# Groups of 6, 7, 6 and 6 destination blocks in an attention layer, and a rearranged passage into it

## The chip, the cores and the metric

The kernel runs on one core of one Trainium2 chip. The metric is the device time of one execution in microseconds. The median of three runs of the kernel before is 1526.83 us (1523.18 to 1527.76).

## What is computed

A graph network with four layers on 3125 nodes of 128 features and 103,125 edges, sorted by destination; behind each layer the input is added back and a layer norm follows. The change is at the passage from layer 0 to layer 1:

```python
# layer 0: a weighted sum over edges
xw = x @ weight
out = relu(segment_sum(edge_val[:, None] * xw[src], dst, N) + b)
x = layernorm(x + out)

# layer 1: attention, 4 heads of 32 features
h = (x @ W).reshape(n, HEADS, C)
a_s = einsum('nhc,hc->nh', h, att_src)
a_d = einsum('nhc,hc->nh', h, att_dst)
e = leaky_relu(a_s[src] + a_d[dst], 0.2)
p = exp(e - segment_max(e, dst)[dst])
alpha = p / (segment_sum(p, dst)[dst] + 1e-16)
out = segment_sum(h[src] * alpha[:, :, None], dst)
out = out.reshape(n, 128) + gat_bias + x @ skip_W + skip_b
x = layernorm(x + layernorm(out) * ln_g + ln_b)
```

Layer 2 is attention without edge features, layer 3 two mean aggregations with dense products.

## The kernel before

The nodes are cut into 25 blocks of 128 (`NB`). A first stage turns the edges into two dense matrices in DRAM, source block by destination block: `wd`, the sums of edge weights in float32, and `f_ctd`, the number of edges in bfloat16. All four layers then run as dense products over these matrices on TensorE.

**The sums of layer 0.** `add0` (L803) takes one source block `i`: it loads the weights of that block for a range of destination blocks into a tile `cw` (up to ten blocks, 640 KB) and adds `cw^T @ xw[i]` onto one accumulator per destination block; four blocks share a PSUM bank. A float32 product counts as two matmuls in the profile. PSUM has eight banks: five (`acc0` to `acc4`) hold the first twenty destination blocks (`Z0`), which are summed while the matrices are still being made; at the end of the stage the loop L931 adds those source blocks that are still missing. Only then are the banks of the stage free, and the last five destination blocks are summed in `left0` and `left1` by the loop at L1192, over all 25 source blocks, from tiles of a pool of its own (`f_tp1`, eight tiles of 320 KB), which lies in SBUF where pools of the first stage lay. `end0` (L818) applies bias, relu and the layer norm to a bank.

**What is hung into that loop.** `marks` lists steps by source block. `scores1(g)` (L1111) turns four blocks of x, multiplies them with the attention vectors into bank `tr_sa` and a second bank, and sends the second result to DRAM (`add_`). `top` copies the scores to SBUF (`heads`, L1127) and finds their maximum; `spread` and `factors` (L1136) make the exponentials of the nodes (`fa`, `fb`, `own1`) from it. `values(b)` (L1156) makes the features of two source blocks: a product, two scalings on DVE (L1165), and a split into three bfloat16 parts (`split3`, L553 to L561: three casts on ACT, two subtractions on DVE), then negations on DVE (L1175). Four calls of `values` stand in the loop, at source blocks 13, 16, 19 and 22; the remaining nine stand in the first pass of layer 1.

**Layer 1.** `IG` (L503) cuts the destination blocks into groups of 4, 7, 7 and 7. For each group and each pair of heads one pass runs over the 25 source blocks. For a source block, `masks` (L1234) makes one 0/1 mask for each head over the group's columns: for one of five a single DVE operation (L1250), for the others a Relu on ACT (L1256) and a minimum on DVE (L1257). `products` (L1261) then issues three matmuls for each destination block, one with the counts (L1267) and two with the masks (L1272). A destination block has a PSUM bank of its own, 402 floats. At the end of a pass `sums` (L1285) reduces each bank on DVE (`nz`, L1291), so the next pass's products into a bank wait for that. `quotients`, `finish1` (two layer norms, gain, bias, and the products that layer 2 needs) and `skips` are put a number of steps later with `later`, one step being one source block; they run beside the masks and products of later passes. For the first group, the banks of layer 0 are used: two of its sums and two of left; for later groups seven banks and one spare.

**The order.** A scheduler arranges the instructions of each engine around the program's order; each engine and each queue runs in its order. SP issues all loads and stores of this stretch from one queue, so a load that waits for a tile holds those behind it.

Of the kernel before, what the change touches and what calls it, by code (L numbers as in the profile page):

```python
# [7 lines left out]
F32 = mybir.dt.float32  # L8
# [7 lines left out]
P = 128  # L16
N = 3125
NB = 25
# [476 lines left out]
NBT = NW // BW  # L495
LW = 4
NL = (NBT - 1) * BW + LW
Z0 = 20
V1 = 100
GA = 80.0  # L500
UP = 2.0**60
GM = 40.0
IG = [(0, 4), (4, 7), (11, 7), (18, 7)]  # L503
QG = [(0, 13), (13, 12)]
LN = N - (NB - 1) * P
GT = [(0, 4), (4, 4), (8, 4), (12, 4), (16, 4), (20, 2), (22, 2), (24, 1)]
# [4 lines left out]
def fast_path(  # L511
# [287 lines left out]
    def bias0(acc, n):  # L799
        for j in range(n):  # L800
            nc.tensor.matmul(acc[:, j, :], ones, l0_br, start=(j == 0), stop=False, skip_group_check=True)

    def add0(pool, i, accs, blocks):  # L803

        b0, n = blocks
        for h in range(0, n, 10):
            m = min(10, n - h)
            cw = pool.tile([P, min(10, n), P], F32, name="cw")[:, 0:m]
            nc.sync.dma_start(
                cw.rearrange("p c d -> p (c d)"), wd[i * P : (i + 1) * P, (b0 + h) * P : (b0 + h + m) * P]  # L810
            )
            for j in range(h, h + m):
                nc.tensor.matmul(  # L813
                    accs[j // 4][:, j % 4, :], cw[:, j - h, :], xw[:, i, :], start=False,
                    stop=(i == NB - 1 and (j % 4 == 3 or j == n - 1)), skip_group_check=True,
                )
# [61 lines left out]
    for b in range(NBT):  # L878
# [49 lines left out]
        while acc0 and (done + 1) * P <= (b - 1) * BW * WN:  # L928
            add0(zp, done, acc0, (0, Z0))
            done += 1  # L930
    for i in range(done, NB):  # L931
        add0(zp, i, acc0, (0, Z0))
    front.close()
    r = xw

# [20 lines left out]
    def later(k, f):  # L956
        due.append((now[0] + k, f))
# [123 lines left out]
    with ExitStack() as st:  # L1081
# [16 lines left out]

        fp = st.enter_context(tc.tile_pool(name="f_fp1", bufs=2))
        tail = ExitStack()  # L1100
        tp = tail.enter_context(tc.tile_pool(name="f_tp1", bufs=8))
        zpp = zero.enter_context(tc.tile_pool(name="f_zpp", bufs=1, space=PSUM))
        left = GB[Z0 // 4 :]
        acc1 = [zpp.tile([P, 4, P], F32, name=f"left{k}") for k in range(len(left))]
        t8 = zpp.tile([P, 512], F32, name="tr_sa")
        for a, (b0, n) in zip(acc1, left):
            bias0(a, n)
        for g in range(Z0 // 4):
            end0(acc0[g], *GB[g])

        def scores1(g):  # L1111

            b0, n = GB[g]
            tag = f"acc{min(g, 2)}"
            turned(zps, xT, b0, n, tag)
            for k in range(n):
                b = b0 + k
                nc.tensor.matmul(
                    t8[:, b * 2 * H : (b + 1) * 2 * H], xT[:, b * P : (b + 1) * P], watt, start=True, stop=True
                )  # L1120
# [6 lines left out]
        def heads(b0, n):  # L1127

            b = slice(b0, b0 + n)
            nc.vector.tensor_copy(  # L1130
                sa[:, b, :], t8[:, b0 * 2 * H : (b0 + n) * 2 * H].rearrange("p (b h) -> p b h", h=2 * H)
            )
            nc.vector.tensor_scalar(nas[:, b], sa[:, b, 0:H], -1.0, None, OP.mult)
            nc.gpsimd.tensor_scalar(bas[:, b], sa[:, b, 0:H], UP, None, OP.mult)

# [41 lines left out]
                )  # L1177

        spare.append(lambda: zps.tile([P, 512], F32, name="few", tag="acc1"))
        marks = {3: lambda: scores1(0), 4: lambda: (scores1(1), scores1(2)), 5: lambda: scores1(3), 6: lambda: scores1(4)}  # L1180
        keep = {}

        def top():
            heads(0, Z0)
            ex = fp.tile([P, H], F32, name="ex", bufs=1)
            nc.vector.tensor_reduce(ex, sa[:, 0:Z0, 0:H].rearrange("p b h -> p h b"), AX.X, OP.max)
            keep["d"] = highest(fp, ex, H)

        marks[7] = top
        marks[9] = lambda: (spread(keep["d"], H, km), factors(0, Z0))  # L1190
        ready = 0
        for i in range(NB):  # L1192
            add0(tp, i, acc1, (Z0, NB - Z0))
            if i in marks:
                marks[i]()
            if i >= 13 and i % 3 == 1:
                values(ready)
                ready += 2
        tail.close()
# [85 lines left out]
        def sums(acc, g, hp):  # L1285
# [469 lines left out]
```

## Time and profile before

| | |
|---|---|
| median of three runs | 1526.83 us |
| the profiled execution | 1523.26 us |
| its span, first to last instruction | 1521.5 us |
| TensorE busy | 1387.3 us, 91% |
| DVE busy | 975.9 us, 64% |
| ACT busy | 903.8 us, 59% |
| last product of the edge matrices (L901) | starts at 468.1 us |
| last product of the first twenty sums | ends at 498.2 us |
| maximum of the scores known (`km`) | 528.45 us |
| last product of left | starts at 544.1 us |
| first product of layer 1 | 546.6 us |
| reductions `nz` of the eight passes begin | 597.4, 627.3, 685.5, 732.1, 793.6, 841.9, 903.3, 955.1 us |
| first products of scores in layer 2 (L1408) | 962.0 us |

PE is TensorE's matmul side, PEld its weight loads, DVE, ACT and POOL the other engines, SPq the queue that issues DMAs. In a row of a stretch the columns are the stretch, its length, and for each engine its busy time with the number of instructions; then the granted TensorE clock as a share of full speed, the share of time that the 16 DMA engines were busy, and the rate. In a row of the timeline the start, the duration, engine, line and operation, output<-inputs and the count are given; brackets hold the idle time before it and what ended it. In a row of a group, busy time and the mean of one follow the first bar, and idle time before it with its causes follows the second.

### The profile page before, as it was taken

To read this page: it belongs to the slowest core of one execution; us is meant where nothing else is said; L and a number is where in the kernel's file an instruction comes from. 1 tells how busy PE (TensorE), PEld (TensorE's weight loads), DVE (VectorE), ACT (ScalarE), POOL (GpSimd) and SP (SyncE) were. 2 spreads that over 40 slices of the span, in tenths; PEclk is the share of its full clock that TensorE was granted. 3 is DMA by queue.
4 is the path that set the end of the run, shared out by engine and by line. 5 is a ranking of instruction groups with operands and counts; after the bars stand their busy time and mean duration, and the time that the engine had idled before them with its cause. 6 is when DMAs were issued, how large, how long until landed. Compare 5 with 4: busy or idle time off the path is not lost. (4 is left out here: it accounts for less than half of the span.)

```text
span 1521.5 us, 35026 instructions
## 1 busy us (share of the span) xinstructions
PE 1387.3 (91%) x14762; PEld 1214.9 (80%) x14775; DVE 975.9 (64%) x1595; ACT 903.8 (59%) x1845; POOL 129.3 (8%) x164
## 2 busy tenths in 40 slices
PE   2898999999997987899989989899999999999994
PEld 2898999899897776889979979677777774458994
DVE  5989999989990389869978878544464351012006
ACT  2878887878882479878778677454465331023003
POOL 2000000000000023113212311300000000000000
PEclk9999999999999999999999999999999999999997
DMA  6478787877888633444434433332222216513651
GB/s 172 125 194 217 211 225 189 241 200 208 230 229 253 201 101 98 143 122 123 133 117 120 130 92 104 123 111 68 68 61 78 80 62 251 200 36 133 199 191 46
DMA packets 209702, 223.92 MB, mean 147 GB/s; under 512 B 72956, under 2 KB 183339, under 8 KB 209277
## 3 DMA queue, kind: packets, MB, share of 16 engines
q1 hardware_dynamic: 208748, 218.51, 49.5%
q8 instruction: 117, 1.92, 0.5%
q0 software_dynamic: 400, 1.97, 0.4%
q10 hardware_dynamic: 385, 1.11, 0.3%
q14 instruction: 52, 0.43, 0.1%
HBM read 157.19 MB, written 64.36 MB: 146 GB/s over the span
## 5 line engine op out<-in xcount | busy, mean ns | idle before, releaser
L1272 PE MATMUL acc<-vp,cm 128*128 128x198 bf16 x2500 | 343.2, 252 | 7.3 <-DVE cm L1257 4.6
L1256 ACT ACTIVATE fm<-adr,bas 128x896 bf16<-128x896 f32 (+1 forms) x320 | 286.0, 952 | 66.6 <-DVE cm L1257 61.9
L1267 PE MATMUL acc<-vp,ct 128*128 128x204 bf16 x1250 | 314.1, 255 | 8.3 <-DVE vp L1175 4.5
L1272 PEld LDWEIGHTS <-cm 128*128 128x128 bf16 x2500 | 235.1, 98 | 25.2 <-DVE cm L1257 8.6
L901 PE MATMUL wp<-wod,ohc 128*128 128x128 bf16 x3768 | 242.1, 220 | 10.0 <-ACT cs L906 5.5
L901 PEld LDWEIGHTS <-ohc 128*128 128x128 bf16 x3768 | 222.0, 98 | 11.9 <-issue 11.6
L862 DVE TENSOR_TENSOR wod<-ohd,w 128x4096 bf16<-128x4096 bf16 (+2 forms) x122 | 221.3, 1867 | 0.6 <-PE wp L901 0.6
L1257 DVE TENSOR_TENSOR cm<-fm,ct 128x896 bf16<-128x896 bf16 (+1 forms) x320 | 196.7, 644 | 36.1 <-PE acc L1272 13.8
L868 ACT ACTIVATE wod<-ohd,wu 128x128 bf16<-128x128 bf16 x628 | 194.5, 399 | 0.0
L1412 DVE TENSOR_TENSOR e<-e,ct 128x416 f32<-128x416 f32 (+1 forms) x175 | 108.2, 625 | 106.8 <-ACT e L1411 99.3
L1411 ACT ACTIVATE e<-s,f_nm 128x416 f32<-128x416 f32 (+1 forms) x175 | 109.5, 632 | 98.4 <-PE s L1408 91.3
L1416 PEld LDWEIGHTS acc<-self__8021,e 128*128 128x128 f32 x1250 | 148.5, 193 | 20.5 <-issue 18.5
L1416 PE MATMUL acc<-self__8021,e 128*128 128x129 f32 x1250 | 149.0, 276 | 0.5 <-DVE e L1412 0.5
L1408 PE MATMUL s<-yT,f_xT 128*128 128x416 f32 (+1 forms) x350 | 142.6, 542 | 4.6 <-ACT rt L1388 4.0
L813 PE MATMUL acc<-f_xw,cw 128*128 128x128 f32 x1000 | 119.4, 279 | 8.0 <-DMA cw<-wd 8.0
L1267 PEld LDWEIGHTS <-ct 128*128 128x128 bf16 x1250 | 122.2, 98 | 2.4 <-issue 1.5
L813 PEld LDWEIGHTS acc<-f_xw,cw 128*128 128x128 f32 x1000 | 115.4, 194 | 8.8 <-DMA cw<-wd 8.8
L912 ACT COPY ws<-wp 128x512 f32<-128x512 f32 x157 | 91.5, 583 | 48.7 <-PE wp L901 43.2
L893 PE MATMUL cp<-ohc,ohd 128*128 128x125 bf16 x1256 | 96.7, 219 | 23.9 <-ACT ws L912 14.7
L851 DVE TENSOR_TENSOR ohd<-kd,ramp 128x4096 bf16<-128x4096 bf16 (+1 forms) x41 | 90.0, 2196 | 28.2 <-PE cp L893 27.9
L1408 PEld LDWEIGHTS s<-yT,f_xT 128*128 128x128 f32 x350 | 62.3, 191 | 55.4 <-issue 39.4
L1591 PEld LDWEIGHTS <-ct 128*128 128x128 bf16 x1875 | 104.9, 98 | 0.0
(301 smaller groups left out, 1483.8 us busy)
## 6 DMA issues: line engine op xcount, KB each, us to landing
ct<-f_ctd SPq DMA_DIRECT2D x48, 800.0 KB
wd<-ws SPq DMA_DIRECT2D x39, 896.0 KB
ct<-f_ctd SPq DMA_DIRECT2D x150, 224.0 KB
cw<-wd SPq DMA_DIRECT2D x50, 640.0 KB
f_ctd<-cs SPq DMA_DIRECT2D x20, 1000.0 KB
ct<-f_ctd SPq DMA_DIRECT2D x25, 416.0 KB
ct<-f_ctd SPq DMA_DIRECT2D x25, 365.2 KB
cw<-wd SPq DMA_DIRECT2D x25, 320.0 KB
```

What stands on the lines that cost most here:

```text
L813: nc.tensor.matmul(accs[j // 4][:, j % 4, :], cw[:, j - h, :], xw[:, i, :], start=False, stop=(i == NB - 1 and (j % 4 == 3 or j == n - 1)) ...
L862: nc.vector.tensor_tensor(packed(f, ww), packed(ohd, ww), twos(w2[s])[:, ww], OP.mult)
L868: nc.scalar.activation(wod[2][:, BW + w, :], ohd[:, BW + w, :], AF.Copy, scale=w3[:, 1, at : at + 1])
L901: made = nc.tensor.matmul(wp[:, j, :], ohc[:, w, :], wod[s][:, w, :], start=(j == 0 and q == 0 and s == 0), stop=(j == 3 and q == 1 and s ...
L1256: nc.scalar.activation(f[:, : n * P], at, AF.Relu, bias=bas[:, c, h : h + 1], scale=UP)
L1257: nc.vector.tensor_tensor(m[:, : n * P], f[:, : n * P], ct[:, : n * P], OP.min)
L1267: nc.tensor.matmul(out_(F1, PW), ct[:, k * P : (k + 1) * P], vp[:, c, hp : hp + 2, :, 2 * F1 : V1], start=(c == 0), stop=False, skip_group ...
L1272: nc.tensor.matmul(out_(0, 2 * F1)[:, j], ms[j][:, k * P : (k + 1) * P], vp[:, c, hp + j, :, 0 : 2 * F1], start=False, stop=(c == NB - 1 a ...
L1408: nc.tensor.matmul(s[:, :m], xT[:, c * P : (c + 1) * P], yT[:, i0 * P + a : i0 * P + a + m], start=True, stop=True)
L1411: nc.scalar.activation(e[:, a : a + m], s[:, :m], AF.Exp, bias=nm[:, q : q + 1], scale=scale)
L1412: nc.vector.tensor_tensor(e[:, a : a + m], e[:, a : a + m], ct[:, a : a + m], OP.mult)
L1416: nc.tensor.matmul(acc[k // 3][:, (k % 3) * (P + 1) : (k % 3 + 1) * (P + 1)], es[q, c][:, k * P : (k + 1) * P], vo[:, c, 0 : P + 1], start ...
```

## The change

- The groups are 6, 7, 6 and 6. The first group takes six banks: `acc3`, `acc4`, `acc2`, `tr_sa` and the two of left.
- `add0` gets the width of a tile as a parameter. The missing source blocks of the first twenty sums (23 and 24, since the loop of the stage reaches 22) are added after the stage's pools are closed, from tiles of five blocks of `f_tp1`. That pool is placed on the other side of SBUF.
- Ahead of these two source blocks the first five source blocks of left are added (`ZA`), and the loop over left begins at the sixth.
- The marks move up by five source blocks, so that they have the same distance from the loop's new begin. `values` runs at every source block from 16 on: nine calls instead of four.
- The scores of the last five blocks go to the bank `acc0` instead of `tr_sa`, and `heads` for them runs within `scores1`.
- The quotients of the first group come seven steps after the pass instead of four.

```diff
+ZA = 5
-IG = [(0, 4), (4, 7), (11, 7), (18, 7)]
+IG = [(0, 6), (6, 7), (13, 6), (19, 6)]
...
-    def add0(pool, i, accs, blocks):
+    def add0(pool, i, accs, blocks, w=10):
...
-        for h in range(0, n, 10):
-            m = min(10, n - h)
-            cw = pool.tile([P, min(10, n), P], F32, name="cw")[:, 0:m]
+        for h in range(0, n, w):
+            m = min(w, n - h)
+            cw = pool.tile([P, w, P], F32, name="cw")[:, 0:m]
...
-    for i in range(done, NB):
-        add0(zp, i, acc0, (0, Z0))
     front.close()
...
-        tp = tail.enter_context(tc.tile_pool(name="f_tp1", bufs=8))
+        tp = tail.enter_context(tc.tile_pool(name="f_tp1", bufs=8, side="right"))
...
         for a, (b0, n) in zip(acc1, left):
             bias0(a, n)
+
+        for i in range(done, NB - 2):
+            add0(tp, i, acc0, (0, Z0), 5)
+        for i in range(ZA):
+            add0(tp, i, acc1, (Z0, NB - Z0), 5)
+        for i in range(max(done, NB - 2), NB):
+            add0(tp, i, acc0, (0, Z0), 5)
...
-            tag = f"acc{min(g, 2)}"
+            tag = f"acc{min(g, 2) if b0 < Z0 else 1}"
             turned(zps, xT, b0, n, tag)
+            t, a = (t8, b0) if b0 < Z0 else (zps.tile([P, 512], F32, name="tr_s", tag="acc0"), 0)
...
+            if b0 >= Z0:
+                heads(t, b0, n)
...
-        marks = {3: lambda: scores1(0), 4: lambda: (scores1(1), scores1(2)), 5: lambda: scores1(3), 6: lambda: scores1(4)}
+        marks = {8: lambda: scores1(0), 9: lambda: (scores1(1), scores1(2)), 10: lambda: scores1(3), 11: lambda: scores1(4)}
...
-        marks[7] = top
-        marks[9] = lambda: (spread(keep["d"], H, km), factors(0, Z0))
+        marks[12] = top
+        marks[14] = lambda: (spread(keep["d"], H, km), factors(0, Z0))
...
-        for i in range(NB):
-            add0(tp, i, acc1, (Z0, NB - Z0))
+        for i in range(ZA, NB):
+            add0(tp, i, acc1, (Z0, NB - Z0), 5)
             if i in marks:
                 marks[i]()
-            if i >= 13 and i % 3 == 1:
+            if i >= 16:
                 values(ready)
                 ready += 2
...
-        later(7, lambda: (heads(Z0, NB - Z0), factors(Z0, NB - Z0)))
+        later(7, lambda: factors(Z0, NB - Z0))
...
-            later(1 if last else 4, quotients)
+            later(1 if last else 4 if g else 7, quotients)
...
-                    acc = [zps.tile([P, 512], F32, name="acc1", tag=f"acc{3 + k}") for k in range(2)]
-                    acc += [zpp.tile([P, 512], F32, name="acc1", tag=f"left{k}") for k in range(2)]
+                    acc = [zps.tile([P, 512], F32, name="acc1", tag=f"acc{k}") for k in (3, 4, 2)]
+                    acc += [zpp.tile([P, 512], F32, name="acc1", tag=k) for k in ("tr_sa", "left0", "left1")]
```

More of the change, by code (lines that the diff above doesn't have):

```diff
@@ L1113, in scores1 @@
             b0, n = GB[g]
-            tag = f"acc{min(g, 2)}"
+            tag = f"acc{min(g, 2) if b0 < Z0 else 1}"
             turned(zps, xT, b0, n, tag)
+            t, a = (t8, b0) if b0 < Z0 else (zps.tile([P, 512], F32, name="tr_s", tag="acc0"), 0)
             for k in range(n):
-                b = b0 + k
                 nc.tensor.matmul(
-                    t8[:, b * 2 * H : (b + 1) * 2 * H], xT[:, b * P : (b + 1) * P], watt, start=True, stop=True
-                )
+                    t[:, (a + k) * 2 * H : (a + k + 1) * 2 * H], xT[:, (b0 + k) * P : (b0 + k + 1) * P], watt,
+                    start=True, stop=True,
+                )
+            if b0 >= Z0:
+                heads(t, b0, n)
             t = zps.tile([P, 512], F32, name="tr_ad", tag=tag)
@@ L1125, in scores1, with heads @@
             nc.sync.dma_start(add_[:, b0 * P : (b0 + n) * P], ad[:, : n * P])
-        def heads(b0, n):
+        def heads(t, b0, n):
             b = slice(b0, b0 + n)
-            nc.vector.tensor_copy(
-                sa[:, b, :], t8[:, b0 * 2 * H : (b0 + n) * 2 * H].rearrange("p (b h) -> p b h", h=2 * H)
-            )
+            nc.vector.tensor_copy(sa[:, b, :], t[:, 0 : n * 2 * H].rearrange("p (b h) -> p b h", h=2 * H))
             nc.vector.tensor_scalar(nas[:, b], sa[:, b, 0:H], -1.0, None, OP.mult)
@@ L1179, in fast_path @@
         spare.append(lambda: zps.tile([P, 512], F32, name="few", tag="acc1"))
-        marks = {3: lambda: scores1(0), 4: lambda: (scores1(1), scores1(2)), 5: lambda: scores1(3), 6: lambda: scores1(4)}
+        marks = {8: lambda: scores1(0), 9: lambda: (scores1(1), scores1(2)), 10: lambda: scores1(3), 11: lambda: scores1(4)}
         keep = {}
         def top():
-            heads(0, Z0)
+            heads(t8, 0, Z0)
             ex = fp.tile([P, H], F32, name="ex", bufs=1)
```

## The prediction

> **What bounds the kernel now.** I read the page's busy shares first, then busy time by stretch, with the stretches cut at the places where the change acts, then the timeline of TensorE in the passage, then the mask operations by shape. All times are of the profiled execution.
>
> ```profile
> span 1521.5 us, 35026 instructions
> PE 1387.3 (91%) x14762; PEld 1214.9 (80%) x14775; DVE 975.9 (64%) x1595; ACT 903.8 (59%) x1845; POOL 129.3 (8%) x164
> ```
>
> TensorE is busy 91% of the span, so a gain must come out of the other 9%, about 134 us, or out of work that disappears. No matmul disappears here. So I ask where TensorE waits.
>
> ```profile
> core 0: us, PE busy (x) PEld busy (x) DVE busy (x) ACT busy (x) POOL busy (x), PEclk, DMA share, GB/s
> 468.40:498.20 29.80, 21.68 (x171) 20.91 (x170) 3.67 (x22) 2.24 (x4) 1.45 (x2) 0.94 0.81 253
> 498.20:528.50 30.30, 29.07 (x199) 22.89 (x200) 9.67 (x51) 13.60 (x33) 0.43 (x1) 0.94 0.70 223
> 528.50:546.60 18.10, 16.76 (x150) 16.59 (x150) 12.49 (x33) 9.14 (x18) 4.74 (x17) 1.00 0.54 159
> 546.60:597.40 50.80, 40.19 (x351) 33.53 (x352) 47.57 (x140) 48.19 (x89) 13.48 (x25) 0.93 0.29 86
> 597.40:627.30 29.90, 28.03 (x308) 26.82 (x307) 27.34 (x68) 27.11 (x42) 5.38 (x7) 1.00 0.46 134
> 627.30:685.50 58.20, 50.88 (x530) 48.74 (x529) 42.99 (x93) 47.00 (x65) 10.54 (x11) 0.97 0.43 128
> 685.50:732.10 46.60, 45.83 (x523) 45.59 (x521) 41.51 (x61) 37.39 (x40) 11.90 (x7) 1.00 0.47 136
> 732.10:793.60 61.50, 53.75 (x556) 50.88 (x554) 49.87 (x108) 47.18 (x68) 15.23 (x10) 0.97 0.39 117
> 793.60:841.90 48.30, 47.61 (x535) 46.93 (x533) 43.22 (x65) 38.06 (x47) 11.33 (x8) 1.00 0.45 130
> 841.90:903.30 61.40, 53.41 (x551) 50.46 (x549) 49.39 (x109) 47.46 (x70) 15.22 (x10) 0.97 0.36 102
> 903.30:955.10 51.80, 48.15 (x537) 47.12 (x535) 41.74 (x65) 31.94 (x41) 10.96 (x8) 1.00 0.34 96
> ```
>
> The rows from 546.6 on are the eight passes of layer 1 (two head pairs for each of four groups), cut where the reductions nz of a pass begin. The first pass (four blocks) has 300 products and takes 50.8 us; DVE and ACT are both busy for some 48 us of it, so these two bound it, with the features (`values`) on top of the masks. The pass 685.5 to 732.1 is bound by TensorE: 525 products in 46.6 us, 0.088 us each, 6.6 us for a block. Passes in which the group before is being finished (58.2, 61.5, 61.4) take 12 to 15 us over that rate.
>
> ```profile
> 471.68 4.73 PE L813 MATMUL acc<-f_xw,cw 128*128 128x128 f32 x40 [1.17 <-DMA cw<-wd]
> 479.00 4.73 PE L813 MATMUL acc<-f_xw,cw 128*128 128x128 f32 x40 [2.59 <-DMA cw<-wd]
> 487.36 10.83 PE L813 MATMUL acc<-f_xw,cw 128*128 128x128 f32 x80 [3.62 <-DMA cw<-wd]
> ...
> 503.53 6.61 PE L813 MATMUL left<-f_xw,cw 128*128 128x128 f32 x50
> ```
>
> The last four source blocks of the first twenty sums wait 7.4 us for their counts; then TensorE mostly idles between 498.2 and 503.5, since SP issued the first load for the five left blocks only at 498.21, when the last reader of the older buffers was through. A full-speed round of left is 10 matmuls of 0.113 us.
>
> ```profile
> L1257 DVE TENSOR_TENSOR cm<-fm,ct 128x896 bf16<-128x896 bf16 x240 | 164.2, 714 | 32.8 <-PE acc L1272 11.8 <-ACT fm L1256 9.5 <-issue 4.5
> L1250 DVE SCALAR_TENSOR_TENSOR cm<-adr,nas,ct 128x896 bf16<-128x896 f32 x60 | 74.9, 1248 | 6.4 <-PE acc L1272 6.3
> L1257 DVE TENSOR_TENSOR cm<-fm,ct 128x512 bf16<-128x512 bf16 x80 | 32.6, 435 | 3.2 <-PE acc L1272 2.0 <-ACT fm L1256 1.1
> L1250 DVE SCALAR_TENSOR_TENSOR cm<-adr,nas,ct 128x512 bf16<-128x512 f32 x20 | 15.7, 786 | 0.7 <-PE acc L1272 0.5 <-DMA ct<-f_ctd 0.2
> L1256 ACT ACTIVATE fm<-adr,bas 128x896 bf16<-128x896 f32 x240 | 233.6, 1032 | 64.1 <-DVE cm L1257 59.5 <-DVE mv L994 3.3 <-DVE ms L1004 0.9
> L1256 ACT ACTIVATE fm<-adr,bas 128x512 bf16<-128x512 f32 x80 | 52.4, 711 | 2.5 <-DVE cm L1257 2.4
> ```
>
> These masks overlap when they stand back to back; from start to start the timeline gives 0.33 and 0.54 us (L1257 at 512 and 896 columns), 0.66 and 1.07 (L1250), 0.61 and 0.93 (L1256). At 768 columns I interpolate 0.47, 0.93 and 0.83.
>
> **What the Trainium skill says.** "TensorE: Matmul & The Clock Gate" (Part 1) says that an idle window of about 3.4 us halves the clock, and that about 3.4 us of work restores it. The trace agrees: the granted clock falls to 0.94 and 0.93 in the stretches with waits and is 1.00 in the pass without. "PSUM — Partial Sum Buffer" (The four PSUM rules) says that a matmul's output stays within one bank; a block here takes 402 floats, so six blocks need six banks, and two of these come late: tr_sa and the second left. "DMA: Bandwidth & Descriptors" (Queues, rings and completion order) says each DMA engine consumes descriptors in ring order; the trace agrees as far as 470 to 490 shows 343 and 302 GB/s at a share of 1.03, so loads put ahead push others back. "ScalarE: Activation LUTs" (What ACT_TABLE_LOAD costs) prices an ACTIVATE with a pointer operand at 280 ns + 0.833 ns per column, less 93 ns back to back, 827 ns at 768 columns, an estimate that fits my 0.83.
>
> **The change part by part.**
>
> *Five rounds of left moved ahead of blocks 23 and 24.* Their loads are 5 x 320 KB = 1.6 MB, 4.8 us at 343 GB/s, in a stretch where DMA is full; they can't fill the waits for free. Block 23's first 640 KB let TensorE start at 487.4; a tile of half the size does so at about 486.5. Then 50 matmuls (5.7 us) and 80 (9.1 us), with the DMA now ahead: the first twenty sums end at about 501.3 instead of 498.2, with five rounds done. Loads go on meanwhile, since the pool now lies on the other side and has eight tiles for both uses; the idle behind 498.2 goes. SP issues eight loads for blocks 23 and 24 instead of four: 4 x 0.43 us of issue, hidden behind 1.1 us of TensorE for each tile (1.7 us if not).
>
> *Scores and maximum.* From the order of the built instructions, 70 matmuls of left stand between that end and km, where 62 stood, and two of values have moved up. 140 x 0.113 (two passes each) = 15.8, five scores of 2.6 (transposes 0.5, two kinds of products 1.06 and 1.02) = 13, values 0.5: 29.3. km stands at about 531 instead of 528.45, with six rounds of left still to do instead of twelve or thirteen. The DMAs of add_ stand in SP's queue behind loads that wait for tiles, and ACT's next copy of ad waits for them; each has 2 to 3 us of TensorE work to hide in, and costs up to 2 if that is short. The counts of the first masks no longer wait for the last tiles of left (1.35 us at 546.6 before); DVE is later than that now, so nothing comes of it. The last two scores copy their heads themselves: one copy and one negation more on DVE, 0.4 us, in the sum below, and one small operation on POOL, which is idle.
>
> *Nine pairs of features before the first mask instead of four.* One pair costs DVE 2.4 us net (two v 0.33, two subtractions 0.68 and 0.64, two negations 0.22) and ACT 1.7. The built order puts all nine, and nearly all of the norm of the left banks, ahead of the first mask on DVE. Start 2.4, nine pairs 21.6, norm and first mask about 4: first masked products at 531 + 28 = 559 instead of 549.4. TensorE has 30 matmuls of left (6.8) and 18 of values (4.5) for these 28 us and idles some 17.
>
> *First pass with six blocks.* TensorE: 450 x 0.088 = 39.5, features of the last seven blocks 1.8, second scores 3.0: 44.3, plus 1.7 for a half clock of 3.4 us behind the idle time. DVE: 42 x 0.47 + 10 x 0.93 = 29.0, four pairs 9.6, the rest (factors, copies, norm) 3.8: 42.4. So TensorE and DVE are almost level, and ACT is not far off; I add 1.5 for their waits on each other (0 to 6 possible). End: 559 + 47.5 = 606.5 instead of 597.4, **9.1 us later**.
>
> *The other seven passes.* They hold 44 block passes instead of 46: 2 x 6.6 = 13.2 us less. Finishing costs, over the TensorE rate, 12.2 us for four blocks and 15.4 for seven, so 1.1 a block on a fixed 7.8: groups of 6, 7, 6 give 14.4 + 15.5 + 14.4 less 0.5 for fewer skips = 43.8 against 43.1. The finish of the first group starts three steps later (quotients after 7, not 4) and spills into its next pass; the three spills I price at 1.7 more. Sum **-10.8** (-13 to -6).
>
> *The end.* Six banks to reduce instead of seven before layer 2 (one nz, 0.57) and one block less to finish beside it (0.6): **-1.2**.
>
> Sum: 9.1 - 10.8 - 1.2 = -2.9. The profiled execution took 1523.26 us (span 1521.5), which would become 1520.4; it lies 3.6 under the median of the runs, 1526.83, from which I get 1524.
>
> **The rivals.** (a) *The new order hides more than I say*: features and masks mesh without waits, the clock does not fall, the passes finish at the old extra cost. First products at 557, pass of 44.5, end 601.5 (+4); rest -13; end -1.2: -10, 1517. For it: DVE had only 3 us of idle in the pass 546.6 to 597.4. Against: three engines over 90%. (b) *Slower: the features become a chain.* ACT has to do five masks (0.83 each) among the last features, and a pair's three casts and two subtractions alternate between ACT and DVE; if a pair takes 3.3 us instead of 2.4, nine take 8.1 longer, TensorE idles 25 us and nothing later gives it back: -2.9 + 8.1 = +5.2, 1532. It decides from a pair of 2.4 + 2.9/9 = 2.7 us on. For it: single-file, the chain v to negation is about 5 us (530.85 to 535.7 in the trace). Against: the built order interleaves two pairs. (c) *It does not fill the waits at all*, because DMA is full: then the sums end 3 us later still, 1527, no change.
>
> **How the numbers follow.** My forecast 0.45, (a) 0.28, (b) 0.17, (c) 0.10. A measurement of this kernel tells apart about 0.3%, 4.6 us. Faster by more: most of (a), and the better third of my own case, 0.27 + 0.15 = 0.42. Slower by more: most of (b), little of the others, 0.17. Between: 0.41. Range: the low end takes in (a) and its spread, the high end (b): 1515 to 1533.
>
> **What would show it.** Right: no wait for cw over 3 us behind the first left load; km near 531; a hole of about 17 us in TensorE before products at 559; nz of the first pass at 606; the other passes at about 44, 60, 48, 55, 42, 54 and 44 us. Wrong: nz before 602 (then masks and features mesh better) or after 611 (the features are a chain), or finishing passes that cost more than 16 us over the rate.

## The result, and the profile after

The kernel after takes 1527.74 us in the median of 12 runs (1525.62 to 1530.84); the kernel before, in 12 runs between them, 1525.43 us (1522.25 to 1528.16). The ratio is 1.0019, 95% interval 1.0011 to 1.0028: slower by 2.9 us, a small but resolved loss. The profiled execution of after took 1530.31 us, that of before 1523.26. This pair is 7.0 us apart, more than the medians, because the one lies 2.6 above its median and the other 2.2 below. So places are read from the profiles, and sizes of a few microseconds from the ratios. The edge matrices are done at another time in each profile (their last product starts at 468.2 us in before and 469.0 in after); where that matters I count from there.

First the busy shares of after, then busy time by stretch, cut at the same events as for before: last product of the edge matrices, first product of left, end of the first twenty sums, `km`, first masked product, and then the beginning of each pass's reductions.

```profile
span 1528.5 us, 35039 instructions
PE 1386.7 (91%) x14762; PEld 1217.6 (80%) x14775; DVE 984.3 (64%) x1597; ACT 905.7 (59%) x1845; POOL 129.0 (8%) x165
```

```profile
469.20:492.30 23.10, 12.51 (x92) 11.95 (x91) 0.09 (x2) 1.87 (x2) 1.45 (x2) 0.88 0.93 279
492.30:509.30 17.00, 17.00 (x132) 17.00 (x133) 3.48 (x19) 0.33 (x2) 0.00 (x0) 0.86 0.91 302
509.30:538.00 28.70, 28.59 (x218) 23.90 (x218) 9.73 (x51) 13.47 (x33) 0.43 (x1) 1.00 0.60 190
538.00:566.20 28.20, 13.33 (x99) 11.69 (x98) 27.59 (x73) 22.35 (x38) 12.01 (x30) 0.74 0.17 57
566.20:614.50 48.30, 46.54 (x473) 44.03 (x474) 42.80 (x100) 45.47 (x69) 5.64 (x13) 0.94 0.41 115
614.50:657.20 42.70, 40.66 (x450) 39.52 (x448) 38.41 (x73) 35.20 (x42) 8.14 (x7) 1.00 0.43 124
657.20:717.60 60.40, 52.83 (x546) 49.58 (x544) 48.08 (x101) 47.36 (x65) 14.64 (x10) 0.97 0.42 121
717.60:768.20 50.60, 48.16 (x534) 47.12 (x533) 43.34 (x65) 38.13 (x48) 10.35 (x8) 1.00 0.43 120
```

TensorE's busy time in the span is the same as before to 0.6 us (1386.7 and 1387.3). The whole difference is waiting. In the first row TensorE idles 10.6 of 23.1 us; in the fourth it idles 14.9 of 28.2 us while DVE is busy all but 0.6 us. The remaining four passes take 57.1, 45.2, 53.8 and 40.9 us.

| us, profiled executions | before | predicted | after |
|---|---|---|---|
| first product of left | 503.5 | 486.5 | 492.3 |
| end of the first twenty sums | 498.2 | 501.3 | 509.3 |
| `km` | 528.45 | 531 | 538.0 |
| first masked product | 549.4 | 559 | 566.2 |
| first `nz` of the first pass | 597.4 | 606.5 | 614.5 |
| the other seven passes together | 357.7 | 346.9 | 350.6 |
| from the last pass's `nz` to the end of the span | 566.4 | 565.2 | 563.4 |

The difference of 7.0 is 17.1 us up to the first `nz`, less 7.1 in the seven passes, less 3.0 behind. The prediction lost its 8 us ahead of the end of the first twenty sums (0.8 of them because the matrices were done later in this execution); from there to the first `nz` it has 105.2 us, and 105.2 were measured. Here is TensorE's timeline of that place (start, duration, operation, count, and in brackets the idle time ahead of it):

```profile
472.52 4.73 PE L814 MATMUL acc<-f_xw,cw 128*128 128x128 f32 x40 [1.20 <-DMA cw<-wd]
479.85 6.36 PE L814 MATMUL acc<-f_xw,cw 128*128 128x128 f32 x40 [2.60 <-DMA cw<-wd]
492.28 8.06 PE L814 MATMUL left<-f_xw,cw 128*128 128x128 f32 x50 [6.08 <-issue]
500.17 9.10 PE L814 MATMUL acc<-f_xw,cw 128*128 128x128 f32 x80
```

The wait ahead of block 23 (3.6 us before) has not gone: it stands ahead of left and is 6.08 us long, though left's tiles are half the size. "issue" there means that TensorE waited for nothing that the view could name. So I looked at who issues the load: SP's timeline, of before and of after.

```profile
475.82 0.38 SPq L917 DMA_DIRECT2D f_ctd<-cs  x1
476.44 23.99 SPq L809 DMA_DIRECT2D cw<-wd  x9
```

```profile
476.82 0.53 SPq L918 DMA_DIRECT2D f_ctd<-cs  x1
486.24 1.29 SPq L1251 DMA_DIRECT2D ct<-f_ctd  x3
487.64 4.36 SPq L810 DMA_DIRECT2D cw<-wd  x8
```

Before, SP went from the last store of the counts (`f_ctd<-cs`) to the next load of weights in 0.24 us; there it waited 5.2 us for TensorE to have read an older tile. After, it stands still from 477.35 to 486.24, issues three loads of counts for the first masks of layer 1, and only then the loads of weights. SP's waits in after name what the loads of counts waited for (total, times, longest):

```profile
SPq L1251 <- PE acc L814: 4.8, 1, 4.8
SPq L1251 <- DMA cw<-wd: 3.8, 2, 2.3
```

They waited for the last loads into the stage's weight tiles and then for TensorE's last product from these, which ends at 486.21. The addresses of the built kernel fit this: the pool of the counts' tiles lies at 170752 to 181504 bytes of each partition, and the first weight tile of the stage at 179552 to 184672. They did not wait for the store of the counts ahead of them, as two of the expectations below take it; the run with the pool at another place shows this. In the order of the built instructions they stood ahead of left's loads; I had looked there for matmuls and for operations of DVE, not for SP's.

The masks by shape, as the last part: from start to start, back to back, the timeline gives 0.469, 0.926 and 0.826 us for L1264, L1257 and L1263 at 768 columns; I had interpolated 0.47, 0.93 and 0.83.

### The profile page after: what moved, and what is told of

Same layout as the page of the kernel before. It is cut to its first block, busy times and chain, and to the rows that moved or that the text cites. A ratio compares the mean times of both kernels' runs of the same rounds, so it can differ in the third digit from the quotient of the medians.

```text
span 1528.5 us, 35039 instructions
## 1 busy us (share of the span) xinstructions
PE 1386.7 (91%) x14762; PEld 1217.6 (80%) x14775; DVE 984.3 (64%) x1597; ACT 905.7 (59%) x1845; POOL 129.0 (8%) x165
## 4 chain that ended last, share of the span: by engine, by line
PE 70%; ACT 11%; DVE 10%; issue 3%; DMA 3%; POOL 2%; SPq 0%; ACTq 0%; DVEq 0%; POOLq 0%
PE acc L1279 9%; PE wp L902 9%; PE acc L1423 9%; PE s L1415 8%; PE acc L814 7%; PE acc L1522 6%; PE acc L1598 6%; PE acc L1274 5%; ACT wod L869 4%; PE cp L894 3%; DVE cm L1264 3%; ACT ws L913 2%; ACT fm L1263 1%; PE left L814 1%; DVE nz L1298 1%
## 5 line engine op out<-in xcount | busy, mean ns | idle before, releaser
L1263 ACT ACTIVATE fm<-adr,bas 128x768 bf16<-128x768 f32 (+1 forms) x320 | 286.9, 952 | 63.3 <-DVE cm L1264 60.6
L1279 PEld LDWEIGHTS <-cm 128*128 128x128 bf16 x2500 | 235.7, 98 | 22.6 <-DVE cm L1257 10.3
L902 PEld LDWEIGHTS <-ohc 128*128 128x128 bf16 x3768 | 222.7, 98 | 10.8 <-issue 10.5
L1264 DVE TENSOR_TENSOR cm<-fm,ct 128x768 bf16<-128x768 bf16 (+1 forms) x320 | 202.1, 662 | 33.4 <-PE acc L1279 17.7
L1598 PEld LDWEIGHTS <-ct 128*128 128x128 bf16 x1875 | 104.9, 98 | 0.0
```

The costliest lines, as they stand in the source:

```text
L902: made = nc.tensor.matmul(wp[:, j, :], ohc[:, w, :], wod[s][:, w, :], start=(j == 0 and q == 0 and s == 0), stop=(j == 3 and q == 1 and s ...
L1263: nc.scalar.activation(f[:, : n * P], at, AF.Relu, bias=bas[:, c, h : h + 1], scale=UP)
L1264: nc.vector.tensor_tensor(m[:, : n * P], f[:, : n * P], ct[:, : n * P], OP.min)
L1279: nc.tensor.matmul(out_(0, 2 * F1)[:, j], ms[j][:, k * P : (k + 1) * P], vp[:, c, hp + j, :, 0 : 2 * F1], start=False, stop=(c == NB - 1 a ...
L1598: nc.tensor.matmul(acc[g][:, j, :], ct[:, (b0 + j) * P : (b0 + j + 1) * P], ups[b // 4][:, b % 4, s, :], start=(b == 0 and s == 0 and j == ...
```

## The experiments

My theory after this reading: the loads of the moved rounds are late, by SP's order or by something else that they wait for, and the 28 us of features ahead of the first mask are paid without a return. The rivals: the DMA engines are full there, so nothing that SP does helps (the prediction's third rival); the groups themselves cost the loss; the wait is the features' alone. All ratios are to the kernel before. The experiments ran in three sets (rows 2 to 5, 6 to 9 and 10 to 13 of the table), each with the kernel before beside it; an expectation that speaks of a first or second run means one of its own set.

| kernel | median, us | ratio | 95% interval |
|---|---|---|---|
| after | 1527.74 | 1.0019 | 1.0011 to 1.0028 |
| counts held back | 1525.58 | 1.0000 | 0.9991 to 1.0008 |
| groups alone | 1525.21 | 1.0002 | 0.9992 to 1.0011 |
| held, old groups | 1523.39 | 0.9991 | 0.9983 to 0.9999 |
| held, four pairs | 1522.58 | 0.9978 | 0.9970 to 0.9986 |
| other place | 1527.14 | 1.0013 | 1.0003 to 1.0024 |
| other place, held | 1524.04 | 0.9995 | 0.9986 to 1.0004 |
| other place, held, four pairs | 1519.97 | 0.9968 | 0.9952 to 0.9984 |
| other place, held, no rounds moved | 1523.99 | 0.9993 | 0.9986 to 1.0000 |
| one pool, held | 1522.66 | 0.9989 | 0.9979 to 1.0000 |
| one pool, held, four pairs | 1518.95 | 0.9963 | 0.9948 to 0.9978 |
| the same, old groups | 1521.04 | 0.9970 | 0.9962 to 0.9979 |
| the same, quotients after 4 | 1519.13 | 0.9963 | 0.9952 to 0.9974 |

**Counts held back.** The first six loads of counts are put on SP behind the last load of left, `loaded` being that load:

```diff
-            add0(tp, i, acc1, (Z0, NB - Z0), 5)
+            loaded = add0(tp, i, acc1, (Z0, NB - Z0), 5)
...
-                masks(*items[y_])
+                if y_ < 6:
+                    with tc.issue_after(loaded.ins):
+                        masks(*items[y_])
+                else:
+                    masks(*items[y_])
```

> The changed kernel with one order put right: the first six loads of counts for layer 1 are queued on SP behind the last load for the five left blocks, everything else as changed. Theory (a queue blocked on SP): in the changed kernel three of these loads stand ahead of the left loads and hold them until the last store of the counts has landed; without that, left begins near 486.5 instead of 492.3, the first twenty sums end near 501.5 instead of 509.3, km comes near 531 instead of 538.0, the first nz near 607 instead of 614.5, and the time is 0.9965 of the kernel before (against 1.0019 for the changed kernel). Rival (the passage is covered: features on DVE or the transfer of the weights set the pace anyway): the first nz stays within 2 us of 614.5 and the ratio stays at 1.002.

Left did not start earlier: 492.94 us, 0.7 later than in after. Counted from the last product of the matrices that is 23.5 us, against 23.3 in after; the two other kernels with this passage and held counts (old groups, four pairs) show 22.3 and 21.9, so single profiles of this passage scatter by 1.6 us, and no gain shows. But with the counts out of the way SP's own waits now name what is behind them. The first fence is SP's timeline of this kernel, the second its waits (total, times, longest):

```profile
479.03 0.43 SPq L919 DMA_DIRECT2D f_ctd<-cs  x1
489.82 2.23 SPq L810 DMA_DIRECT2D cw<-wd  x5
```

```profile
SPq L810 <- DMA wd<-ws: 5.5, 1, 5.5
SPq L810 <- DMA f_ctd<-cs: 4.7, 1, 4.7
```

The load of left's first tile itself waits for the last stores of the stage, 10.4 us in all from the end of the store's issue. The addresses of the built kernel say why: the new pool lies at 208864 to 229344 bytes of each partition, over the second buffer of `cs` (202912 to 210912) and over `ws` (210912 to 227296), the tiles from which these stores read. The program makes a load into such a place wait for the store from it. In before, blocks 23 and 24 used the weight tiles that the stage itself had turned over; their loads waited for TensorE and for earlier loads, not for a store. The theory that SP's order alone was at fault falls. The kernel gained 0.0019 all the same (and 0.0018 at the other place, below). The profiles of both pairs show where some of it comes from: `km` follows the end of the first twenty sums after 27.3 us instead of 28.7, a stretch in which TensorE is busy throughout and does one round of left, ten matmuls, fewer. The hold has moved that round behind `km`, where TensorE waits for the features anyway. That is 1.4 of the 1.7 and 1.8 us that the two pairs gain from there to the first `nz`. In the first pair another 1.8 us lie in the seven passes, in the second nothing, but there left starts 1.7 us earlier as well. What the seven passes gain stays open.

**The groups alone.** On the passage of before, only the groups, the six banks, the scores' heads and the later quotients are changed:

```diff
-IG = [(0, 4), (4, 7), (11, 7), (18, 7)]
+IG = [(0, 6), (6, 7), (13, 6), (19, 6)]
```

> The groups alone: 6, 7, 6 and 6 blocks, six banks for the first, heads of the last blocks within their scores and quotients after seven steps, but the sums, marks and the places of the features as before. Theory (the groups gain what the sum said, the passage lost it): the first pass grows by about the 9 us that DVE has more in masks, first nz near 607, the other seven passes are 7 to 11 us shorter in sum, the end 2 to 3 us shorter: ratio 0.998. Rival (the groups themselves cost, since features and larger masks fall into the same pass): first nz later than 613 and a ratio over 1.001.

Ratio 1.0002. The first `nz` comes at 606.35 instead of 597.42 (+8.9), the seven passes are 5.2 shorter, the rest 1.9 shorter. The groups shift work and neither gain nor lose by themselves: the first `nz` came as the theory said and the end nearly so, the seven passes gained less than its 7 to 11 us, and neither its ratio nor the rival's was met. And the mirror of it, the new passage (held) with the old groups:

> The passage alone with the loads of counts held back as in the first run of this call, groups of 4, 7, 7 and 7. Theory: km near 531, DVE then has the nine pairs of features ahead of the masks and the first pass is bound by DVE as before, so the first nz comes near 596, 1 to 2 us earlier than before, and the ratio is 0.999. Rival (nine pairs ahead of the first mask cost by themselves): first nz later than 602 and a ratio over 1.003.

0.9991, against 1.0000 with the new groups: intervals that overlap. The first `nz` came at 599.12, between the two expectations, and the ratio was the theory's. The groups are not what was lost.

**Four pairs of features ahead instead of nine**, on the kernel with the counts held:

```diff
-            if i >= 16:
+            if i >= 18 and i % 2 == 0:
                 values(ready)
```

> As the first run of this call, but only four pairs of features stand ahead of the first pass (at source blocks 18, 20, 22 and 24), the other nine in it, as in the kernel before. Theory (DVE's total decides, not where the features stand): the first masked product comes some 12 us earlier, the hole of 20 us in TensorE shrinks to under 8, but the first pass becomes longer by as much, first nz within 2 us of the first run of this call. Rival (the hole is the loss): first nz 5 us or more earlier than in the first run of this call, ratio lower by 0.003.

Ratio 0.9978 against 1.0000: 3.4 us. In the profile the first masked product comes at 551.62 instead of 565.68, 14.1 us earlier, and the first `nz` at 606.99 instead of 613.24, 6.2 earlier: more than half of the features' time comes back as a longer first pass, the rest is a net gain. The rival is right in the place; its 0.003 was somewhat too much.

**The pool at another place.** An unused tile of 26,432 bytes per partition ahead of it puts `f_tp1` at 182432 to 202912, over the stage's weight tiles and the first buffer of `cs`:

```diff
+        tail.enter_context(tc.tile_pool(name="f_pad", bufs=1, side="right")).tile([P, 6608], F32, name="pad")
         tp = tail.enter_context(tc.tile_pool(name="f_tp1", bufs=8, side="right"))
```

> The changed kernel with only the place of the weight tiles moved: a pool that is never written stands beside them, so that they no longer lie on the staging buffers cs and ws. In the first call holding back the counts' loads did not bring left forward (492.9 against 492.3): its first load still waited for the stores out of cs and ws, whose memory its tiles cover. Theory (the memory is the wait, and the counts' loads ahead in SP's queue are a second one behind it): left still waits, now for the counts' loads, which need the stored counts; first left matmul near 489 to 492, ratio 1.000 to 1.002. Rival (the memory alone): left begins near 486.5, ratio 0.996.

> The moved tiles and the counts' loads held behind the last load of left. Theory (both waits are gone): left begins near 486.5, when the transfers ahead of it have drained, the first twenty sums end near 502, km near 531, first nz near 607, ratio 0.996. Rival (the transfers themselves set the pace there): left begins near 490 again, ratio 0.999 to 1.000.

> As the run before it, with only four pairs of features ahead of the first pass (source blocks 18, 20, 22, 24). In the first call this put the first masked product 14 us earlier and the first nz 6 us earlier. Theory (the hole in TensorE is a loss that the first pass, now bound by TensorE as well, can't make up): first nz near 600, ratio 0.993. Rival (with the sums earlier DVE is the only bound of the first pass): first nz as in the run before it.

Left starts at 490.34, 489.05 and 489.77 us, which is 22.7, 21.0 and 21.0 us behind the last product of the matrices (23.3, 23.5 and 21.9 without the pad), and the ratios are 1.0013, 0.9995 and 0.9968. That is better than without the pad in each pair (1.0019, 1.0000, 0.9978), but each step is within the intervals. The first of the three kernels settles what the loads of counts wait for: they are issued at 484.21, and the load of weights behind them still waits 1.1 us for the store of the counts, until 486.72. So they do not need that store, and most of the time for which they block SP is time that left's first load would spend waiting for it anyway. In the second kernel SP issued the first load of left at 486.04, again behind that store: a buffer of `cs` still lay below. The waits there name the stores from `ws` too (3.5 us), though the moved pool no longer covers `ws`; why is not shown. So the second run did not take both waits away as its theory had it, and its numbers are the rival's. The third came out between its two expectations: first `nz` at 605.54, 1.8 us earlier than in the second, with a ratio lower by 0.0027.

**No rounds moved** (`ZA = 0`, the marks five source blocks earlier), with the place and the held counts:

> As the second run of this call, but no round of left is moved ahead of source blocks 23 and 24; the marks stand five source blocks earlier, at the same distance from the loop's begin. Theory (loads are in one full queue, so the moved rounds only push the last two blocks back): the first twenty sums end 4 to 5 us earlier than in the second run, km comes 3 us earlier, and the first nz is the same within 2 us, ratio within 0.001 of it. Rival (the moved rounds fill the waits): first nz 3 to 6 us later than in the second run.

0.9993 against 0.9995. From the last product of the edge matrices to the end of the first twenty sums it takes 32.9 us without the rounds and 36.9 with them, for 5.7 us of matmuls moved; to the first `nz` 139.6 and 139.1. The theory is right: the five moved rounds push the last two blocks back by 4.0 us, and gain half a microsecond up to the first `nz` in the profile, which the medians don't show.

**One pool for all of it.** The wait for the stores can be taken away: one pool of six tiles, opened ahead of the stage, used for the stage's own source blocks as well, so that no store reads from where a weight tile lies:

```diff
+    tail = ctx.enter_context(ExitStack())
+    tp = tail.enter_context(tc.tile_pool(name="f_tp1", bufs=6, side="right"))
     front = ctx.enter_context(ExitStack())
...
-    zp = front.enter_context(tc.tile_pool(name="f_zp", bufs=3))
...
-            add0(zp, done, acc0, (0, Z0))
+            add0(tp, done, acc0, (0, Z0), 5)
```

> The kernel after, with one pool of six 320 KB weight tiles opened ahead of layer 0's stage and used in the stage's loop, for the last first-twenty sums, for left and to the end of the passage (the stage's own three 640 KB tiles are gone), and with the first six counts loads put on SP behind the last left load. Theory that the loads for the last source blocks wait for stores of the staging tiles because a new pool lies over these: here no load waits for anything but TensorE's reading of an older tile, SP issues the first load for the moved rounds at 477 to 480, left starts at 486 to 488, the first twenty sums end at 501 to 503, nz of the first pass comes at 603 to 606, ratio 0.998 to 0.9995. Rival, that the DMA queues are full and in order, so that the tile can't land sooner whatever SP does: left starts at 489 or later as in the run with the pool at another place, sums end at 505, ratio 0.9995 or above.

The timeline of SP in this kernel and its waits for TensorE, then two rows of TensorE's timeline (source blocks 21 and 22, then left), then the stretch that ends where left begins:

```profile
477.73 0.48 SPq L920 DMA_DIRECT2D f_ctd<-cs  x1
478.30 14.01 SPq L812 DMA_DIRECT2D cw<-wd  x8
```

```profile
SPq L812 <- PE acc L816: 7.7, 7, 4.2
```

```profile
471.49 12.09 PE L816 MATMUL acc<-f_xw,cw 128*128 128x128 f32 x80 [1.80 <-DMA cw<-wd]
487.86 7.45 PE L816 MATMUL left<-f_xw,cw 128*128 128x128 f32 x50 [4.27 <-DMA cw<-wd]
```

```profile
469.20:487.90 18.70, 12.63 (x86) 12.25 (x84) 0.00 (x0) 0.36 (x1) 0.00 (x0) 0.82 1.08 317
```

SP comes to left's first load 0.09 us behind the store instead of 10.3 (in after, where the counts come first). But the load does not go out there: it is the one that waits 4.2 us, until 482.5, for TensorE to have read an older tile. Blocks 21 and 22 took 12.09 us at a low clock (0.54 from 473 to 478), where 80 such matmuls at full speed take 9.10. Then TensorE waits 4.27 us for the load, with the DMA engines at a share of 1.08 throughout; from 483 to 488 they moved 312 GB/s at 1.13 here, and 128 GB/s at 0.63 in after, whose loads were held back. Both sides were partly right: with the wait for the stores gone, left starts 4.4 us earlier than in after (1.6 of which because the matrices were done earlier in that execution) and the ratio falls from 1.0019 to 0.9989. What is left is the rival's, with TensorE's own pace beside it: up to 488 the engines are full with the store and the loads ahead. Whether more tiles than six would bring the load forward was not tested. The first twenty sums end at 504.24, not at 501 to 503, and the first `nz` comes at 607.53, outside of the 603 to 606 that I expected. Against the other place with held counts the gain is small: left starts 20.5 us behind the matrices instead of 21.0, and 0.9989 against 0.9995 is within the intervals.

**One pool with four pairs, and what the groups are worth there.**

> The same with only four pairs of features ahead of the first mask. Both theories: the hole of TensorE before the first masked product shrinks by 12 to 15 us of which about half is given back in the first pass. If the early loads gain as well, ratio 0.995 to 0.9965; if the DMA sets the pace, 0.9965 to 0.998 as with the pool at another place and four pairs (0.9968).

> The same passage (one pool, held counts, four pairs) with the old groups of 4, 7, 7, 7. If the groups are neutral, as in the run of groups alone: equal to the run with the new groups to 0.001. If the new groups gain my predicted 12 less 9 us once the features are not in the way: 0.0015 to 0.003 above it. First pass shorter by 8 to 9 us, seven others longer by 6 to 10, end longer by 1 to 3.

0.9963 with the new groups and 0.9970 with the old ones. With four pairs the hole ahead of the first masked product shrinks by 12.7 us, and 8.2 of these come back in the first pass, as both theories had it. The first is the fastest kernel of the study, 1518.95 us, 6.7 under before; the groups' part in that, 0.0007, is inside the intervals, as for neutral groups, though the medians lie 2.1 us apart. In the profiles the new groups' first `nz` is 6.7 us later (3.2 of it because the matrices were done later in that execution), the seven passes are 6.6 us shorter (350.0 and 356.6) and layer 2 is 2.9 us shorter. So the groups may gain one to two microseconds in this passage, which is not resolved; on the passage of before they gain none.

**Quotients after four steps**, as in before, instead of seven:

```diff
-            later(1 if last else 4 if g else 7, quotients)
+            later(1 if last else 4, quotients)
```

> The same passage with the new groups, and the quotients of the first group after 4 steps of the pass behind it as in the kernel before, not after 7. My prediction priced the spills of the later finish at 1.7 us: ratio 0.001 lower than with 7, seven passes shorter by 1 to 2 us. Rival: DVE is level with TensorE in that pass and the place of the quotients does nothing: within 0.0006.

Seven steps are not a matter of choice with six blocks: in this kernel `skips` writes the last blocks of the first group after the first head pair's quotients were added to them, so that share is lost for these blocks. The instructions are the same ones, so its time can be compared. 0.9963 and 0.9963: no difference. The finish's spill moves and does not go: the pass of seven blocks behind it takes 47.44 us instead of 50.67, and the two passes ahead take 45.53 and 59.39 instead of 43.92 and 58.67. The rival of this run is right in its number; its reason, that DVE is level with TensorE there, is not tested.

## Why the prediction was wrong, point by point

**The step that failed** is *Five rounds of left moved ahead of blocks 23 and 24*, in its sentence "Block 23's first 640 KB let TensorE start at 487.4; a tile of half the size does so at about 486.5." It reckoned with bytes alone. Left started at 492.28, 5.8 us later, and its 50 matmuls took 8.06 us instead of 5.7, since TensorE's clock was down after the wait (0.60 of full speed from 493 to 498): together 8.2 us, where the sums' end missed by 8.0. Two things stood between, both of them memory that the stage had used: a pool in a new place, over staging tiles whose stores its first load had to wait for, and three loads of counts ahead on SP's queue, whose own pool touches the stage's weight tiles. The second hides behind the first: holding back the counts alone did not bring the start forward. Counted from the last product of the matrices, the forecast of 486.5 is 18.3 us; after has 23.3, the four one-pool kernels 20.3 to 21.7, and block 23 in before 19.2, with a tile of twice the size. So of the 5.0 us that the step missed by this count, some 2.8 are the two waits. The other 2.2 stayed with both gone: even without them the half tile came no earlier than the whole one in before. The prediction priced four more issues on SP (1.7 us) and noted in passing that "the pool now lies on the other side", as a gain, though it had itself read a load in before that waited for "the last reader of the older buffers". (Its 7.4 us of waits "for their counts" are waits for weights, `cw`, as its own lines show.) Its sign for a chain of features, a first `nz` after 611, came true at 614.5 for this other reason.

**The third rival, that DMA is full, was half of the truth** and I gave it 0.10. In after the engines were not full when it counted (0.63 from 483 to 488). In the one-pool kernel, without the wait for the stores, they were, and the sums end at 504.24. The rival said 504.3, but the match is partly luck: the matrices were done 0.8 us earlier in that profile than in before's. "DMA: Bandwidth & Descriptors" (Queues, rings and completion order) of the Trainium skill, which the prediction cites for its order by ring, fits the one-pool trace: the load that went out at 482.5 behind the store was of use to TensorE only at 487.86. With the moved rounds' bytes ahead, blocks 23 and 24 go back by 4.0 us of the 5.7 that was moved (the run with no rounds moved).

**Scores and maximum**: 29.3 us from the sums' end to `km` were predicted, 28.7 measured. Right.

**Nine pairs of features**: first masked product at `km` + 28; measured 28.2, with DVE busy for 27.6 of it. The second rival (features as a chain, a pair of 3.3 us) did not occur. The step was right in size; that five of the nine pairs were a poor bargain was in the sum (TensorE idling 17 us; 14.9 measured) and was not drawn out of it. The wait view of TensorE, of after and of the one-pool kernel with four pairs, shows this hole once more: the first matmuls into the last banks of left wait until DVE has read them behind the features.

```profile
PE acc L1274 <- DVE r L821: 9.1, 2, 8.6
```

```profile
PE acc L1274 <- DVE r L824: 5.1, 1, 5.1
```

Three times four pairs gained against nine: 0.0022, 0.0027 and 0.0026, some 3.4 to 4 us.

**First pass**: 47.5 predicted, 48.3 measured. TensorE was busy for 46.5 us of it where I counted 46.0 with the low clock, DVE for 42.8 where I counted 42.4. Right.

**The other seven passes**: -10.8 predicted, -7.1 measured, still within its own range of -13 to -6. The mis-sized terms are TensorE's work, two thirds of the 3.7 us, and its waits, one third. From the stretches, TensorE's busy time fell from 327.7 to 317.0, by 10.7 where I counted 13.2, and its idle time rose from 30.0 to 33.6, by 3.6 where I counted 0.7 + 1.7. The passes were 42.7, 60.4, 50.6, 57.1, 45.2, 53.8 and 40.9 us, where I said 44, 60, 48, 55, 42, 54 and 44: the third to the fifth miss most. The waits of the finish name some of the 3.6:

```profile
PE few L1014 <- ACT f_x L1005: 7.8, 2, 5.9
PE few L1014 <- DVE self__7973 L1020: 6.3, 4, 2.5
```

The same two took 5.8 and 4.1 us before, 4.2 us less; other waits shrank a little. So the groups' sum was 9.1 - 10.8 - 1.2 in the prediction; the groups-alone run gives +8.9 - 5.2 - 1.9 = +1.8 in its profile and no difference in its median. I had set the first term by the new passage, where it is the features that cost 9 us; the groups cost the same 9 us without them.

**The end**: -1.2 predicted, -3.0 measured. From the last pass's `nz` to layer 2 it takes 8.1 us instead of 6.9, where I had counted one reduction less, 0.57 us, as a gain; from the first to the last score product of layer 2 278.9 instead of 281.7. Every profile with the new groups shows 278.3 to 278.9 there and every one with the old groups 281.4 to 281.7, so this goes with the groups, most likely the shorter last one, whose finish runs beside layer 2: 2.8 us where I counted 0.6. The last stretch, from the first product of L1591 (L1598 in after) to the end, takes 125.6 instead of 127.0 and is 125.4 to 126.7 in all other kernels, those with the old groups among them, so the 127.0 belongs to the profiled execution of before.

**The sum**: +8.0 and +3.7 and -1.8 and 0.0 elsewhere are 9.9 us from -2.9 to +7.0 in the profiled executions; in the ratios, from 0.9981 to 1.0019, it is 5.8 us.

**Settled and open.** By ratio, after to one pool (held): -0.0030; nine pairs to four on top: -0.0026; new groups to old: +0.0007, not resolved; moved rounds: 0.0002, not resolved. How the first of these divides between the counts' place in SP's order and the pool's place is only bounded: the order alone gives 0.0019 without bringing left forward, by a round of left behind `km` as far as the profiles show; the place alone gives 0.0006 and one pool over the other place with held counts 0.0006, neither of them resolved.

## What to carry to other kernels

A load that is moved ahead must be followed to its queue and to its buffer: list what stands before it on the queue that issues it, and what last used the memory under its tile. A pool opened over freed buffers makes its first load wait for whatever used them last, here for stores and for TensorE's reads, where tiles that the loop already turns over wait for nothing but their reader (4.2 us here). A wait that is named first can hide a second one behind it: taking away the first alone then shows nothing. And work put ahead of a critical start is paid there in full, while what it saves later is shared with whatever else is busy in that stretch: four pairs ahead beat nine.

## What the runs showed of the hardware

- A store of the counts, 1000 KB, issued at 479.03 and at 477.19 us, held the load that waited for it until 489.82 and 486.04, so 10.8 and 8.9 us from its issue (counts held back, and the same at the other place). I had expected a store to cost its bytes, some 3 us at the 343 GB/s of before.
- Behind a wait TensorE ran for a while at a lower clock: the 50 float32 matmuls of left, 5.7 us at full speed, took 8.06 us behind a wait of 6.08 us in after, and 7.45, 7.25, 8.49 and 7.48 us behind 4.27, 4.40, 5.10 and 3.88 us in the one-pool kernels. It does not follow from the wait's length alone: 40 matmuls of block 22 took 4.73 us behind a wait of 2.59 us in before and 6.36 us behind 2.60 us in after.
- The first five subtractions of L558 in `split3` in after (541 to 552 us) took 1.0 to 1.1 us, the later ones up to the first mask 0.70; POOL's multiplication for `self_` (L1176) ran beside the former. A subtraction of L561 beside it (544 us) was no longer than the others, and I didn't test this.
